# Two graph-attention layers on one core: the opening of the first group reordered, and three smaller edits

## The chip, the cores and the metric

The kernel runs on one core of one Trainium2 chip. The metric is the device time of one execution in microseconds. The profiler calls the engines PE (TensorE, matrix products), DVE (VectorE), ACT (ScalarE), POOL (GpSimd) and SP (SyncE, which here only issues DMAs). PEld is the loading of stationary weights into PE, which overlaps the products.

## The reference, cut to what matters

There are 64 graphs of 256 nodes with 512 features. Each of two layers normalizes, applies a relu, and adds what an attention over the same 256 x 256 adjacency returns.

```python
h = jnp.maximum(_layernorm(x), 0.0)
# layer 0: one head, 512 -> 256, output and h side by side
hw  = h @ W                                       # [64, 256, 256]
e   = leaky_relu(hw @ a[0] + swap(hw @ a[1]), 0.2)
e   = e + -1e9 * (1 - adj)
x   = x + concat([softmax(e) @ hw, hw], axis=-1)
h = jnp.maximum(_layernorm(x), 0.0)
# layer 1: eight heads of 64
q, k, v = h @ Wq.T + bq, h @ Wk.T + bk, h @ Wv.T + bv
s   = where(adj == 0, -inf, q @ k.T / 8)          # per head
x   = x + (softmax(s) @ v) @ Wo.T + bo
```

## The kernel before, in words

All data is float32. The 64 graphs are worked through in 32 groups of two graphs; a group is 512 rows, four strips of 128, two strips per graph. Python unrolls everything, so there are no loops on the chip.

A group passes four stages, each written as a generator whose `yield`s mark places where other work may be put in between.

- `first_norm(g)` takes the statistics of each strip (`st`, `mv`, on DVE), makes the factors `rstd` and `less` (a power and a product on POOL), writes the normalized strips `xn` (ACT, two buffers) and turns them. In the first group PE turns them (`pt`). In later groups DVE transposes 32 x 32 blocks into `xt`, of which there is one buffer, SP stores `xt` to DRAM as `passed`, and four fetches `moved` bring it back with the blocks rearranged. `put` copies the result into `hT0` on ACT.
- `first_layer(g)` multiplies by W with two extra columns for the attention scores (`ph`, copied to `H`), transposes one column of `H` (`pn`), builds the exponentials `e` and masks them with `maskT`, and multiplies by `H` (`po`, four strips). A last column of `H` that holds ones makes the row sums, so a reciprocal `ri` and one combine give the new half of x. Then it takes the statistics of the second normalization strip by strip and turns those strips in the same way, into `hT`; at its end POOL makes four `sums` of quarters of `hT`.
- `project(g)` makes q, k and v. Each is seven half-size products instead of eight (a Strassen-like scheme), so it needs `sums` and, once, sums of the weights (`weight_sums`, four DVE subtractions per matrix). It yields 21 times a group.
- `scores`, `weigh` and `outputs` do the eight-head attention and the last product.

Beside this, once, `judge()` bounds the scores from the inputs: it makes the gram matrices of Wq and Wk (`gram_q`, `gram_k`, 32 matmuls each), squares each three times, sums the squares of the other parameters on ACT, adds all up over the partitions (`total`), and writes one number, `wrong`; SP reads that number at the end of the program and would run a slower version for inputs that fail. `last_bias()` folds the bias of v through Wo into `b_out`, with a wide operand `bv_wide` made on POOL and eight matmuls `pb`; `residual(g)` adds `b_out` to x on POOL.

What sets the order: PE executes its instructions in the order of the program, since every product goes through `in_order` (L129 to L138). On the other engines a scheduler at compile time may move an instruction ahead of earlier ones, by its own model of when operands are ready; `not_sooner` (L121) forbids an instruction to stand ahead of the one written just before it on its engine, and does no more than that. Which piece of which stage is written next to which is fixed by hand: by the driver at L777 to L806 for the opening, where a string of letters says after each of the 21 products of the first group how many pieces of the second group's first layer (`s`) and of the following norms (`n`) come next, and by `steps` (L809) for all later groups. Nearly all instructions show line 35 (the helper that passes them on), 135 (products) or 138 (PE transposes) in the profile, so they are told apart by tile names. PSUM gives five rotating banks to `mm` and three held ones.

Loads of the first three groups' x and of all parameters are issued by SP in program order (L149 to L231). Eight buffers hold x.

Of the kernel before, what the change touches and what calls it, by code (L numbers as in the profile page):

```python
# [8 lines left out]
F32 = mybir.dt.float32  # L9
# [5 lines left out]
P = 128  # L15
# [42 lines left out]
def bounded(  # L58
# [48 lines left out]
    def mm(name):  # L107
        return psum.tile([P, 512], F32, tag="turn", name=name, bufs=5)
# [25 lines left out]
    def matmul(*args, **kwargs):  # L134
        in_order(nc.tensor.matmul(*args, **kwargs))  # L135
# [9 lines left out]
    def load(g, b):  # L145
        xs[g, b] = big.tile([P, NT, D], F32, tag="x", name=f"x{g}_{b}", bufs=8)
        nc.sync.dma_start(xs[g, b], xg[g, b])

    load(0, 0)  # L149
    load(0, 1)  # L150


    ident = const.tile([P, P], F32, name="ident")
    make_identity(nc, ident)

    w0_sb = const.tile([P, HP, F1 + 2], F32, name="w0_sb")
    nc.sync.dma_start(w0_sb[:, :, 2:], w0.rearrange("(c p) o -> p c o", p=P))
    maskT = const.tile([P, NT, N], F32, name="maskT")
    bad = const.tile([P, 2, NT], F32, name="bad")
    a_b = att.tile([P, 2, F1], F32, tag="ps", name="a_b", bufs=1)  # L160
    nc.sync.dma_start(
        a_b, bass.AP(tensor=a0.tensor, offset=a0.offset, ap=[[0, P], [F1, 2], [1, F1]])
    )
    adj_i = att.tile([P, NT, N], I32, tag="e", name="adj_i")
    nc.sync.dma_start(adj_i, adj.rearrange("(t p) k -> p t k", p=P))

    def score_columns():
# [6 lines left out]
                )  # L174

    def mask():
        edge = att.tile([P, NT, N], F32, tag="e", name="edge")
        vector.tensor_scalar(edge, adj_i, 0.0, None, op0=ALU.not_equal)
        pt = mm("pt_mask").rearrange("p (k q) -> p k q", k=NT)
        for kb in range(NT):  # L180
            for t in range(NT):
                transpose(
                    pt[:, kb, t * P : (t + 1) * P], edge[:, t, kb * P : (kb + 1) * P], ident
                )
        vector.tensor_copy(maskT, pt)

        vector.reduce_max(bad[:, 0, :], edge, axis=AX.X)
        vector.tensor_scalar(bad[:, 0, :], bad[:, 0, :], 0.0, None, op0=ALU.is_equal)
        vector.tensor_tensor(edge, edge, adj_i, op=ALU.not_equal)
        vector.reduce_max(bad[:, 1, :], edge, axis=AX.X)  # L190
# [53 lines left out]
    def last_bias():  # L244


        pb = mm("pb")
        b = att.tile([P, 2, 2, P], F32, tag="kept", name="bv_wide")
        for q in range(NQ):
            for half in range(2):  # L250
                gpsimd.tensor_scalar(
                    b[:, half, q, :], ones, bv_col[:, half, q : q + 1], None, op0=ALU.mult
                )
                matmul(
                    pb, b[:, half, q, :], w_sb["o"][:, half, 2 * q : 2 * q + 2, :],
                    start=(q == 0 and half == 0), stop=(q == NQ - 1 and half == 1),
                )
        vector.tensor_add(b_out, pb, b_out)


    def judge():
# [65 lines left out]
        yield  # L327
        yield from squares(2, *[w0_sb[:, c, 2:] for c in range(HP)])
        yield
        total = mm("total")[:, :10]  # L330
        matmul(total, ones, part, start=True, stop=True)
        norm = const.tile([P, 10], F32, name="norm")
# [140 lines left out]
    def first_norm(g):  # L473

        xt = {}
        mv = small.tile([P, GT, 2], F32, tag="mv", name=f"mv0_{g}")
        factors, norm, turn, fetch, put = norm_T(xt, mv, f"0_{g}", g == 0)
        for b in range(GB):
            for t in range(NT):
                xt[b * NT + t] = xs[g, b][:, t, :]  # L480
                stats(mv, xt, b * NT + t, f"0_{g}")
            factors(b)
            yield
            norm(b)
            yield
            turn(b)
            yield
            if g == 0:

                pool, tag, bufs = (big, "hT0", 1) if b == 0 else (att, "moved", 2)  # L490
                hT0[g, b] = pool.tile([P, HP, N], F32, tag=tag, name=f"hT0_{g}_{b}", bufs=bufs)
                put(b, hT0[g, b])
        if g == 0:
            return
        for b in range(GB):
            fetch(b)
        yield
        for b in range(GB):
            hT0[g, b] = big.tile([P, HP, N], F32, tag="hT0", name=f"hT0_{g}_{b}", bufs=1)
            put(b, hT0[g, b])  # L500
            yield

    def first_layer(g):

        xt = [xs[g, b][:, t, :] for b in range(GB) for t in range(NT)]

        H = big.tile([P, GT, F1 + 3], F32, tag="H", name=f"H_{g}", bufs=1)
        gpsimd.memset(H[:, :, F1 + 2 :], 1.0)
        for r in range(GT):
            b, t = divmod(r, NT)  # L510
            ph = mm(f"ph_{g}_{r}")[:, : F1 + 2]
# [28 lines left out]
        for r in range(GT):  # L540
            b, t = divmod(r, NT)
            po = mm(f"po_{g}_{r}")[:, : F1 + 1]
            for kb in range(NT):
                matmul(
                    po, pT[b][:, kb, t * P : (t + 1) * P], H[:, b * NT + kb, 2:],
                    start=(kb == 0), stop=(kb == NT - 1),
                )
            ri = small.tile([P, 1], F32, tag="ri", name=f"ri_{g}_{r}")
            vector.reciprocal(ri, po[:, F1:])
            vector.scalar_tensor_tensor(  # L550
                xt[r][:, :F1], po[:, :F1], ri, xt[r][:, :F1], op0=ALU.mult, op1=ALU.add
            )
            stats(mv, xt, r, f"1_{g}")
            if r == 1:
                factors(0)
            elif r == 2:
                norm(0)
            elif r == 3:
                factors(1)
                if g:  # L560
                    turn(0)
                    fetch(0)
            yield
# [19 lines left out]
    def residual(g):  # L583

        for b in range(GB):
            for t in range(NT):
                xt = xs[g, b][:, t, :]
                not_sooner(gpsimd, "tensor_add", xt, xt, b_out)
# [187 lines left out]

    verdict = judge()  # L777
    norms = (piece for g in range(NG) for piece in first_norm(g))
    for piece in range(5):
        next(norms)  # L780
        if piece == 2:
            score_columns()
    for piece, _ in enumerate(first_layer(0)):
        for _ in range((0, 2, 1, 2, 2, 1)[piece] if piece < 6 else 0):
            next(norms, None)
        if piece == 3:
            mask()
        elif piece == 4:
            next(verdict)
        elif piece == 9:  # L790
            last_bias()
        elif piece == 10:
            next(verdict)
        elif piece == 11:
            weight_sums("q")
    residual(0)
    products, pieces = project(0), first_layer(1) if NG > 1 else iter(())
    for i, parts in enumerate("n s s n s s s s s s s s s s nn nn nn s - - s".split()):
        next(products)
        if i in (1, 8, 15):  # L800
            weight_sums("kvo"[i // 7])
        for part in parts:
            if part != "-":
                next(norms if part == "n" else pieces, None)
        next(verdict, None)
    run(verdict)  # L806

# [402 lines left out]
```

## Time and profile before

| | us |
|---|---|
| median of 5 runs (2545.8 to 2549.89) | 2547.66 |
| the profiled execution, whole | 2549.75 |
| its span, first to last instruction | 2548.0 |
| PE busy in the span | 2511.2 |
| DVE / ACT / POOL busy | 1776.8 / 1006.5 / 956.4 |
| one group in the steady part (start of its first pq to that of the next, 192.10 to 269.39) | 77.3 |

The span is what the profile covers; the whole execution has 1.75 us around it. Busy times are sums over instructions. The opening, up to about 130 us, is where the groups fill the pipeline; after it each group repeats the same order every 77.3 us. Times in the text are microseconds from the span's start. In the prediction a row "A <- B" of a waits view says that A's engine stood idle until B, with the total, the number of times and the longest; in a view by time a row begins with its start and duration, and brackets at its end give the idle time before it and what ended that.

### The profile page before, as it was taken

How to read it: one execution, taken by the hardware profiler on the slowest of the kernel's cores; microseconds unless marked ns; L12 is line 12 of the kernel's file. 1: busy time of each engine (PE TensorE's matmuls, PEld its weight loads, DVE VectorE, ACT ScalarE, POOL GpSimd, SP SyncE). 2: the span in 40 equal slices, each digit the busy share in tenths (PEclk: the TensorE clock that was granted, in tenths of full speed). 3: DMA queues.
4: the chain of work that ended last, by engine and by line, in shares of the span. 5: the costliest groups of instructions: out<-in, count | busy, mean ns of one | idle time of the engine just before them, and what ended most of it. 6: DMA issues, size and time to landing. Idle time of an engine off the chain costs nothing.

```text
span 2548.0 us, 41575 instructions
## 1 busy us (share of the span) xinstructions
PE 2511.2 (99%) x16158; PEld 2029.5 (80%) x16158; DVE 1776.8 (70%) x2975; ACT 1006.5 (40%) x2015; POOL 956.4 (38%) x944
## 2 busy tenths in 40 slices
PE   7899999999999999999999999999999999999998
PEld 5788888887888888888788888878888888887875
DVE  5667667767677776677776677776677676777655
ACT  3444343433433433434433434344334434334321
POOL 2334343333443333443243433334433334432332
PEclk8999999999999999999999999999999999999999
DMA  6111222312323212223212233123233123232110
GB/s 186 61 65 60 90 83 92 100 59 67 100 75 100 91 59 75 92 83 100 78 60 87 83 92 100 59 67 100 75 100 97 56 73 98 77 100 81 37 34 34
DMA packets 129353, 205.40 MB, mean 81 GB/s; under 512 B 13952, under 2 KB 78208, under 8 KB 129152
## 3 DMA queue, kind: packets, MB, share of 16 engines
q1 hardware_dynamic: 129152, 202.69, 25.4%
q8 instruction: 129, 2.11, 0.4%
q14 instruction: 72, 0.59, 0.1%
HBM read 104.08 MB, written 98.57 MB: 80 GB/s over the span
## 4 chain that ended last, share of the span: by engine, by line
PE 96%; DVE 2%; ACT 1%; POOL 1%; DMA 1%; issue 0%; SPq 0%; ACTq 0%; DVEq 0%; POOLq 0%
PE pq L135 15%; PE pv L135 15%; PE pk L135 15%; PE py L135 15%; PE sc L135 10%; PE ph L135 9%; PE pr L135 9%; PE po L135 4%; PE total L135 3%; PE pn L138 1%; DMA x<-in_x_dram 0%; DMA a_b<-in_L_gnn_a_dram 0%; DVE p L35 0%; POOL ps L35 0%; DVE st L35 0%
## 5 line engine op out<-in xcount | busy, mean ns | idle before, releaser
L35 POOL TENSOR_TENSOR ps<-p 128x512 f32<-128x512 f32 x256 | 416.4, 1641 | 697.0 <-DVE p L35 697.0
L35 DVE TENSOR_TENSOR x<-py,x 128x256 f32<-128x256 f32 x448 | 186.5, 416 | 314.1 <-PE py L135 307.4
L35 ACT ACTIVATE p<-sc 128x512 f32<-128x512 f32 x512 | 264.3, 603 | 272.5 <-PE sc L135 272.5
L35 DVE TENSOR_TENSOR p<-p,maskT 128x1024 f32<-128x1024 f32 x256 | 335.7, 1341 | 48.8 <-ACT p L35 48.8
L35 ACT ACTIVATE xn<-x,less,rstd 128x512 f32<-128x512 f32 x256 | 194.9, 812 | 323.0 <-POOL less L35 307.1
L135 PE MATMUL sc<-q,k 64*128 64x256 f32 x2048 | 266.9, 390 | 0.0
L135 PE MATMUL py<-wo_sb,o_sums 128*128 128x256 f32 x1024 | 262.7, 380 | 2.6 <-DVE x L35 2.6
L35 DVE RECIPROCAL r<-total 128x256 f32<-128x256 f32 x128 | 224.7, 1755 | 44.6 <-PE total L135 44.6
L135 PEld LDWEIGHTS sc<-q,k 64*128 64x128 f32 x2048 | 195.9, 186 | 72.2 <-issue 52.6
L135 PE MATMUL ph<-w_sb,hT 128*128 128x258 f32 x1024 | 245.6, 387 | 1.7 <-ACT hT L35 1.3
L135 PE MATMUL pr<-p,v 128*32 128x256 f32 x4096 | 245.5, 379 | 0.0
L135 PE MATMUL pv<-wv_sb,sums 128*128 128x256 f32 x1024 | 241.8, 379 | 1.2 <-ACT kept_v L35 1.2
L135 PE MATMUL pq<-sums,wq_sb 128*128 128x256 f32 x1024 | 238.5, 381 | 3.0 <-POOL sums L35 3.0
L35 POOL TENSOR_TENSOR rstd<-ve,rexp 128x2 f32<-128x2 f32 x128 | 90.1, 704 | 401.7 <-DVE less L35 401.7
L135 PE MATMUL pk<-sums,wk_sb 128*128 128x256 f32 x1024 | 240.2, 382 | 0.0
L135 PEld LDWEIGHTS ph<-w_sb,hT 128*128 128x128 f32 x1024 | 193.3, 192 | 41.1 <-ACT p L35 9.9
L135 PEld LDWEIGHTS pk<-sums,wk_sb 128*128 128x128 f32 x1024 | 191.7, 190 | 35.6 <-issue 10.3
L135 PEld LDWEIGHTS pq<-sums,wq_sb 128*128 128x128 f32 x1024 | 195.2, 191 | 30.3 <-POOL sums L35 3.8
L135 PEld LDWEIGHTS pv<-wv_sb,sums 128*128 128x128 f32 x1024 | 194.5, 190 | 28.0 <-ACT kept_v L35 1.6
L135 PEld LDWEIGHTS py<-wo_sb,o_sums 128*128 128x128 f32 x1024 | 191.9, 190 | 29.1 <-DVE x L35 3.4
L135 PEld LDWEIGHTS pr<-p,v 128*32 128x32 f32 x4096 | 134.6, 110 | 86.7
L135 PE MATMUL py<-wo_sb,oT 128*128 128x256 f32 x768 | 197.0, 380 | 2.5 <-DVE x L35 2.5
(120 smaller groups left out, 3729.1 us busy)
## 6 DMA issues: line engine op xcount, KB each, us to landing
passed<-xt SPq DMA_DIRECT2D x124, 512.0 KB, 2.7
moved<-passed SPq DMA_DIRECT2D x496, 128.0 KB, 3.5
x<-in_x_dram SPq DMA_DIRECT2D x64, 512.0 KB, 4.8
out_dram<-x SPq DMA_DIRECT2D x64, 512.0 KB, 3.8
wq_sb<-in_L_gnn_Wq_dram SPq DMA_DIRECT2D x2, 512.0 KB, 9.7
wk_sb<-in_L_gnn_Wk_dram SPq DMA_DIRECT2D x2, 512.0 KB, 12.5
wo_sb<-in_L_gnn_Wo_dram SPq DMA_DIRECT2D x8, 128.0 KB, 8.6
wv_sb<-in_L_gnn_Wv_dram SPq DMA_DIRECT2D x2, 512.0 KB, 6.3
```

What stands on the lines that cost most here:

```text
L35: instruction = getattr(self.engine, operation)(*args, **kwargs)
L135: in_order(nc.tensor.matmul(*args, **kwargs))
L138: in_order(nc.tensor.transpose(*args))
```

## The change

There are six edits.

1. The load of the second half of the first group's x goes behind those of the score vectors (`a_b`) and of W (`w0_sb`). The adjacency tiles `adj_i` and `edge` use the buffers with the tag "kept" instead of "e".
2. Both grams of `judge()` are written behind the exponentials of the first group, so both are ahead of `po` on PE; before, the second stood after `pb` and the first transposes. `total` comes three steps later.
3. `last_bias()` becomes a generator in three pieces: the wide operand on POOL is written with the grams, `pb` stays behind `po`, and the add to `b_out` comes two pieces later, bound to the order written.
4. The reciprocal of each `po` strip, in all groups, is bound behind the DVE instruction written before it. In the first group that one is a transpose of the second group, or the reciprocal's own predecessor strip.
5. The first `residual` goes from ahead of the first product to behind product 15, and the string that mixes the second and third group's pieces with the products is another one: several first-layer pieces come in pairs, and the third group's norm starts two steps sooner.
6. `H` is one tile for the whole program, and its column of ones is written once instead of once per group.

```diff
     load(0, 0)
-    load(0, 1)
...
-    w0_sb = const.tile([P, HP, F1 + 2], F32, name="w0_sb")
-    nc.sync.dma_start(w0_sb[:, :, 2:], w0.rearrange("(c p) o -> p c o", p=P))
     maskT = const.tile([P, NT, N], F32, name="maskT")
...
-    adj_i = att.tile([P, NT, N], I32, tag="e", name="adj_i")
+
+    w0_sb = const.tile([P, HP, F1 + 2], F32, name="w0_sb")
+    nc.sync.dma_start(w0_sb[:, :, 2:], w0.rearrange("(c p) o -> p c o", p=P))
+    load(0, 1)
+    adj_i = att.tile([P, NT, N], I32, tag="kept", name="adj_i")
...
-        edge = att.tile([P, NT, N], F32, tag="e", name="edge")
+        edge = att.tile([P, NT, N], F32, tag="kept", name="edge")
...
     def last_bias():
-        pb = mm("pb")
-        b = att.tile([P, 2, 2, P], F32, tag="kept", name="bv_wide")
+        wide = att.tile([P, 2, 2, P], F32, tag="kept", name="bv_wide")
         for q in range(NQ):
             for half in range(2):
                 gpsimd.tensor_scalar(
-                    b[:, half, q, :], ones, bv_col[:, half, q : q + 1], None, op0=ALU.mult
-                )
+                    wide[:, half, q, :], ones, bv_col[:, half, q : q + 1], None, op0=ALU.mult
+                )
+        yield
+        pb = mm("pb")
+        for q in range(NQ):
+            for half in range(2):
                 matmul(
-                    pb, b[:, half, q, :], w_sb["o"][:, half, 2 * q : 2 * q + 2, :],
+                    pb, wide[:, half, q, :], w_sb["o"][:, half, 2 * q : 2 * q + 2, :],
                     start=(q == 0 and half == 0), stop=(q == NQ - 1 and half == 1),
                 )
-        vector.tensor_add(b_out, pb, b_out)
+        yield
+        not_sooner(vector, "tensor_add", b_out, pb, b_out)
+        yield
...
         yield from squares(2, *[w0_sb[:, c, 2:] for c in range(HP)])
         yield
+        for _ in range(3):
+            yield
         total = mm("total")[:, :10]
...
+    H = const.tile([P, GT, F1 + 3], F32, name="H")
+    gpsimd.memset(H[:, :, F1 + 2 :], 1.0)
+
     def first_layer(g):
...
-        H = big.tile([P, GT, F1 + 3], F32, tag="H", name=f"H_{g}", bufs=1)
-        gpsimd.memset(H[:, :, F1 + 2 :], 1.0)
...
-            vector.reciprocal(ri, po[:, F1:])
+            not_sooner(vector, "reciprocal", ri, po[:, F1:])
...
+    bias = last_bias()
...
     for piece, _ in enumerate(first_layer(0)):
+        if piece == 4:
+            next(verdict)
+            next(verdict)
+            next(bias)
         for _ in range((0, 2, 1, 2, 2, 1)[piece] if piece < 6 else 0):
             next(norms, None)
         if piece == 3:
             mask()
-        elif piece == 4:
-            next(verdict)
         elif piece == 9:
-            last_bias()
-        elif piece == 10:
-            next(verdict)
+            next(bias)
         elif piece == 11:
+            next(bias)
             weight_sums("q")
-    residual(0)
     products, pieces = project(0), first_layer(1) if NG > 1 else iter(())
-    for i, parts in enumerate("n s s n s s s s s s s s s s nn nn nn s - - s".split()):
+    order = "n s s n ss s s - ss ss s s n n n s n n n - s"
+    for i, parts in enumerate(order.split()):
         next(products)
         if i in (1, 8, 15):
             weight_sums("kvo"[i // 7])
         for part in parts:
             if part != "-":
                 next(norms if part == "n" else pieces, None)
+        if i == 15:
+            residual(0)
         next(verdict, None)
     run(verdict)
```

## The prediction

> **What bounds the kernel now.** I read the engine shares first, then busy time by stretch, then TensorE's waits in the opening, then that stretch in order of time.
>
> The page, engine shares:
>
> ```profile
> PE 2511.2 (99%) x16158; PEld 2029.5 (80%) x16158; DVE 1776.8 (70%) x2975; ACT 1006.5 (40%) x2015; POOL 956.4 (38%) x944
> ```
>
> PE idles 2548.0 - 2511.2 = 36.8 us in all. Busy time by stretch (stretch, its length, then busy us of PE, PEld, DVE, ACT, POOL, granted clock, DMA share, GB/s):
>
> ```profile
> 0.00:8.57 8.57, 0.00 (x0) 0.00 (x0) 2.32 (x10) 2.15 (x3) 1.93 (x14) 1.00 0.69 216
> 8.57:24.00 15.43, 13.70 (x48) 10.13 (x49) 8.30 (x32) 6.38 (x12) 3.84 (x7) 1.00 0.94 288
> 24.00:31.00 7.00, 4.62 (x41) 4.43 (x40) 6.88 (x17) 3.48 (x9) 1.54 (x3) 1.00 0.52 77
> 31.00:39.26 8.26, 5.40 (x17) 4.12 (x17) 6.27 (x21) 1.34 (x2) 1.66 (x5) 0.77 1.03 385
> 39.26:46.00 6.74, 6.67 (x8) 2.34 (x8) 0.12 (x2) 0.00 (x0) 2.59 (x5) 0.52 0.10 38
> 46.00:56.00 10.00, 7.69 (x50) 7.03 (x50) 2.75 (x5) 4.51 (x7) 0.00 (x0) 0.83 0.62 157
> 90.00:130.00 40.00, 32.33 (x147) 26.53 (x146) 24.96 (x67) 19.65 (x48) 15.62 (x17) 0.96 0.34 106
> 130.00:2433.80 2303.80, 2303.80 (x14934) 1866.35 (x14932) 1634.71 (x2701) 928.52 (x1848) 878.71 (x861) 1.00 0.26 81
> ```
>
> From 130 to 2433.8 us PE never idles, and its last 114 us hold the same work either way. So the change can win or lose only in the first 130 us, or by breaking that unbroken stretch. What idles there (PE's waits, 80 to 140 us):
>
> ```profile
> PE total L135 <- DVE part L35: 3.5, 1, 3.5
> PE pq L135 <- POOL sums L35: 3.0, 1, 3.0
> PE pv L135 <- ACT kept_v L35: 1.2, 1, 1.2
> ```
>
> The opening in order of time (start, duration), which shows what blocks the first projection, pq:
>
> ```profile
> 24.88 3.74 PE L135 MATMUL gram_q<-wq_sb 128*128 128x128 f32 x32
> 31.02 5.39 PE L135 MATMUL po<-H,e 128*128 128x257 f32 x16 [2.40 <-DVE e L35]
> 39.26 7.12 PE L135 MATMUL pb<-wo_sb,bv_wide 128*128 128x512 f32 x8 [2.84 <-POOL bv_wide L35]
> 48.69 1.82 PE L138 MATMUL pt<-ident,xn 128*128 128x128 f32 x8 [2.31 <-ACT xn L35]
> 50.30 4.81 PE L135 MATMUL gram_k<-wk_sb 128*128 128x128 f32 x32
> 55.83 1.89 PE L135 MATMUL pq<-hT,wq_sb 128*128 128x256 f32 x8
> ```
>
> And the DMA view of the one `passed` store issued at 29.62 (last number: us from issue to landing):
>
> ```profile
> passed<-xt SPq DMA_DIRECT2D x1, 512.0 KB, 10.0
> ```
>
> pq starts at 55.83, behind the wide product pb, the b_out add (46.41), the second group's transposes (47.02 to 48.31), xn (47.82), pt and gram_k. The store lands 10.0 us after its issue, at 39.6; that row decides the new opening.
>
> **The change part by part.**
>
> *Load order.* Ahead of a_b stand x(0,0) and x(0,1) and w0; afterwards only x(0,0). x(0,0) lands at 4.6, x(0,1) at 5.8, so a_b (10.34 now) and the score columns behind it come about 1.3 us earlier; SP's later loads keep their place and the DMA engines are full anyway (0.94). adj and edge on "kept" free the first e from waiting 2.9 us for the adjacency check. Both speed up only what ends in another wait (next item), so I count zero; bounds -1.3 and +1 (x(0,1) now lands later, and its statistics with it).
>
> *Both grams ahead of po.* gram_k (32 matmuls, 3.74 at full clock by gram_q's row) fills the 2.40 idle; po then starts near 31 as now, but with PE busy before it, at full clock: 16 x 0.26 (1.03 for 4) = 4.1 instead of 5.39. wk landed at 21.6, so nothing is waited for. *bv_wide* (4 x 0.606 on POOL, inputs landed by 27.5) runs before po ends, delaying only POOL's norm factors, which have slack; pb then ends near 39. The b_out add (0.69) moves behind the last factors, where no one waits for it. No gain by itself: the end of this stage is set by DVE.
>
> *Transposes pinned ahead of the reciprocals.* The xt buffer is single: transposes of the second group's second half wait until the store of the first half has landed, 39.6. Now the four reciprocals, ready to run from 32, stand behind that on DVE, and the statistics, factors and xn behind them. From there: transposes 1.29, to 40.9; four strips of reciprocal, combine, statistics and aggregate at 0.21 + 0.59 + 0.73 + 0.09 = 1.62 (starts at 32.16, 32.37, 32.96; statistics to aggregate 4.63 to 5.36, aggregate to reciprocal 36.59 to 36.68), to 47.4; ve and less 0.35; POOL's power and product 1.15 (37.44 to 38.59); xn 1.52; put 1.05; 0.2 of starts: pq at 51.7. Against 55.83: **-4.1**. Bounds by rows: if the store lands in 3.0 us, like the second one, -11; if only with the last x load at 41.9, -1.8.
>
> *Clock.* PE is now idle from about 39 to 46.5. After the idle of 2.31 at 46.38 the clock was 0.50 until about 52.5; each low spell here lasted about 3.4 or 6.9 us. pq therefore starts cold: half of up to 5 us: **+1.5** (0 to +2.5).
>
> *weight sums, residual.* Sums of wq took 4 in 4.77 us beside POOL adds, those of wo 4 in 2.86 alone. The residual (4 adds, 6.76 beside DVE, 4.96 mostly alone) leaves the first place and lands on the second, after product 15. Then DVE pays up to 1.9 more and the third group's rstd waits behind POOL; PE waits for neither directly. Zero; bounds 0 and +1.9. SBUF — State Buffer (section "SBUF: two separate sides") of the Trainium skill says that of a DVE operation with two SBUF inputs and a GpSimd one, the later to start is blocked for the whole instruction. The sums' 1.19 against 0.72 us agree in sign; full blocking would put rstd behind the whole overlap, 6.8 + 4.8 us by these rows, and cost +2 rather than zero.
>
> *Verdict three steps later, pieces in pairs.* `total` waits 3.5 us for ACT's squares (94.22 to 98.3). The squares now follow the xn of the second group's second half, because that piece moved from step 12 to 10. Carrying PE's own durations (1.73 a product, 0.89 a square, 1.74 a ph strip, 0.87 a po strip) from a warm start at 53.2, `total` comes up near 97.1; the reciprocals, behind the wv sums (2.8 us), end near 91.4, xn near 94.3, the squares near 98.3. So 1.4 to 1.9 us of wait remain: **-1.8** (-3.5 to 0).
>
> *Sums of the second group.* put(1) and the sums sat behind the third group's xn on ACT (116.22 to 119). That norm comes two to three steps earlier; by the same carrying, s2 ends at 110.5 to 111.4 and its product comes up at 112 to 113. The 2.98 wait goes, and with it the clock drop behind it: 24 pq matmuls took 7.17 from 122.88, against 24 x 0.2165 = 5.2 at full clock: **-4.7** (-4.7 to 0; the latter if SP's read of the verdict, which held SP 4.6 us from 98.03 with the fetches behind it, keeps its place while the verdict comes later). TensorE: Matmul & The Clock Gate (Part 1) of the Trainium skill puts the drop after an idle window of about 3.4 us. Here 2.40 and 2.98 us of idle were followed by 0.50, while 3.50 us at 95.09 were not, so the rows go against a fixed length; by the rule that item would be -2.98.
>
> *kept_v.* The third group's xn now stands at step 13, ahead of the copy of the first pv. If ACT takes them in that order, the copy waits: today such an order costs 1.19. Zero change; bounds -1.2 and +5.7 (xn ready near 100.7, done 102.2, copy 102.8, against 97.1).
>
> *H set once.* 31 memsets of 0.10 us and their waits (7.3 us in the first group, 0.7 in each other) leave POOL, which nothing on PE awaits: zero. *Pinned reciprocals later:* in the steady period they already follow their predecessors (316.19 behind the k add, 318.69 and 322.55 behind x adds): zero; bounds 0 and +0.68 a group, one such add.
>
> Sum: -4.1 + 1.5 - 1.8 - 4.7 = **-9.1**. The profiled execution took 2549.75 (span 2548.0 and 1.75 around it), 2.1 above the median of 2547.66; it becomes 2540.7, and the median 2538.6, given as 2538.5.
>
> **The rivals.**
> 1. *Everything clears.* total, kept_v and sums wait nowhere and pq is warm: -4.1 - 3.5 - 1.2 - 4.7 = -13.5: 2534.2. For it: the waits are single events with slack of a few us. Against: the squares' order.
> 2. *A new wait for an old one.* ACT blocks kept_v behind xn: -9.1 + 5.7 = -3.4: 2544.3. For it: xn waited for POOL 3.71 at 106.84 with kept_v behind it. Against: kept_v is not pinned and may be placed ahead.
> 3. *Slower: the pin breaks the steady stretch.* If a pinned reciprocal holds a PSUM bank for one more add, 0.68 x 31 = 21.1 - 9.1 = +12: 2559.7. It turns the sign from 0.29 us a group on. Against: the order just read, and DVE at 70%.
> 4. *Nothing happens, near 2546:* the store lands after 43.7 and the waits merely move. Against: all loads are down by 41.9.
>
> **How the numbers follow.** A measurement of this kernel can tell about 0.2%, 5.1 us, from no change. Forecast 0.45, rival 1 0.20, rival 2 0.15, rival 3 0.12, rival 4 0.08. Faster: 0.45 + 0.20 and a little of rival 2, 0.67; same: the rest of rival 2 and rival 4, 0.20; slower 0.13. Range 2533 to 2548: it takes in rival 1, 2 and 4 and leaves out rival 3 and the far low end.
>
> **What the next profile would show.** Right: gram_k directly after gram_q, po without a wait of 2.4; xt transposes near 39.6 with DVE idle before them, released by `passed`; the first reciprocal after 40.9; pq near 51.7 and cold; `total` waiting under 2 us; no wait of pq for sums; a period of still 77.3. Wrong: transposes well before or after 39.6, a wait at pv above 2 us, any PE wait after 130 us.

## The result and the profile after

The changed kernel takes 2542.85 us (median of 21 runs, 2540.44 to 2544.50); the kernel before took 2548.36 beside it (41 runs). The ratio is 0.9977, 95% interval 0.9971 to 0.9983, so 5.9 us less, between 4.3 and 7.4. The forecast was 9.1 less. The profiled execution has a span of 2542.9 against 2548.0; both profiled executions are slower than their medians (2544.78 and 2549.75).

The page of the changed kernel, engine shares:

```profile
PE 2506.2 (99%) x16158; PEld 2027.6 (80%) x16158; DVE 1771.2 (70%) x2975; ACT 1006.5 (40%) x2015; POOL 954.3 (38%) x913
```

PE now idles 2542.9 - 2506.2 = 36.7 us, as much as before (36.8). The products are the same, so PE is busy 5.0 us less because, on balance, less of them runs at half clock. Busy time by stretch (stretch, its length, then busy us of PE, PEld, DVE, ACT, POOL, granted clock, DMA share, GB/s):

```profile
38.00:46.90 8.90, 0.00 (x0) 0.00 (x1) 6.07 (x18) 0.87 (x2) 0.92 (x2) 0.77 0.83 273
46.90:52.00 5.10, 3.37 (x15) 2.97 (x16) 4.64 (x10) 2.93 (x5) 1.16 (x2) 0.50 0.33 66
52.00:57.00 5.00, 5.00 (x19) 4.16 (x18) 0.00 (x0) 2.12 (x6) 3.66 (x3) 0.55 0.00 0
90.00:100.00 10.00, 7.61 (x28) 6.05 (x27) 7.28 (x25) 5.97 (x19) 1.80 (x4) 0.83 0.23 82
130.00:2433.80 2303.80, 2303.80 (x14919) 1866.92 (x14912) 1637.28 (x2704) 929.50 (x1848) 875.22 (x832) 1.00 0.26 81
```

The last row is the unbroken stretch: 2303.80 of 2303.80 us, and a group still takes 77.3 us (187.22 to 264.52). From about 130 us on the two executions differ by 0.3 us; all else lies ahead of that. There PE does nothing at all for 8.9 us ahead of 46.90, then works at 0.50 and 0.55 of the clock, and drops again between 90 and 100. What it waits for up to 140 us:

```profile
PE pt L138 <- ACT xn L35: 20.4, 4, 9.1
PE pk L135 <- ACT kept_k L35: 2.4, 1, 2.4
PE total L135 <- DVE part L35: 1.1, 1, 1.1
PE pv L135 <- DVE v L35: 0.4, 1, 0.4
PE pq L135 <- POOL sums L35: 0.2, 1, 0.2
```

And the row of the kernel before that the forecast does not show:

```profile
PE pt L138 <- ACT xn L35: 10.9, 2, 8.6
```

`total` fell from 3.5 to 1.1, `sums` from 3.0 to 0.2, kept_v is gone (1.2); a wait of 2.4 for kept_k is new, and PE's wait for xn grew from 10.9 to 20.4 (8.6 and 8.2 of it stand at the very start of the span, for the first load of x). The same in order of time:

```profile
23.56 3.74 PE L135 MATMUL gram_q<-wq_sb 128*128 128x128 f32 x32
27.13 3.74 PE L135 MATMUL gram_k<-wk_sb 128*128 128x128 f32 x32
30.70 3.64 PE L135 MATMUL po<-H,e 128*128 128x257 f32 x16
34.18 3.60 PE L135 MATMUL pb<-wo_sb,bv_wide 128*128 128x512 f32 x8
46.90 1.97 PE L138 MATMUL pt<-ident,xn 128*128 128x128 f32 x8 [9.13 <-ACT xn L35]
50.59 1.97 PE L138 MATMUL pt<-ident,xn 128*128 128x128 f32 x8 [1.73 <-ACT xn L35]
52.35 3.67 PE L135 MATMUL pq<-hT,wq_sb 128*128 128x256 f32 x8
...
57.04 1.89 PE L135 MATMUL pq<-hT,wq_sb 128*128 128x256 f32 x8
...
93.94 3.68 PE L135 MATMUL pk<-hT,wk_sb 128*128 128x256 f32 x8 [2.39 <-ACT kept_k L35]
...
128.64 0.64 PE L135 MATMUL total<-ps,ones 128*32 128x256 f32 x8
```

The first pq starts 3.48 us earlier than before (55.83) but takes 3.67 in place of 1.89, and the second pq is only 1.41 ahead (58.45 before). The last row is the first group's softmax sums, which share the name `total`: 133.44 before, so 4.80 is gained by then, and the spans differ by 5.1. The ledger of these two executions: up to the second pq -1.41, of which 1.32 is there already when gram_q starts (24.88 before, 23.56 now); `total` -2.39; kept_v to v -0.84; sums -2.76 and the clock drop behind them -1.8; kept_k +2.39 and the half clock behind it +1.79. That is -5.02.

### The profile page after: what moved, and what is told of

Same layout as the page of the kernel before. It is cut to its first block, busy times and chain, and to the rows that moved or that the text cites. A ratio compares the mean times of both kernels' runs of the same rounds, so it can differ in the third digit from the quotient of the medians.

```text
span 2542.9 us, 41535 instructions
## 1 busy us (share of the span) xinstructions
PE 2506.2 (99%) x16158; PEld 2027.6 (80%) x16158; DVE 1771.2 (70%) x2975; ACT 1006.5 (40%) x2015; POOL 954.3 (38%) x913
## 4 chain that ended last, share of the span: by engine, by line
PE 95%; DVE 1%; DMA 1%; POOL 1%; SPq 0%; ACT 0%; issue 0%; DVEq 0%; ACTq 0%
PE pq L135 15%; PE pk L135 15%; PE pv L135 15%; PE py L135 15%; PE sc L135 10%; PE ph L135 9%; PE pr L135 9%; PE po L135 4%; PE total L135 3%; PE pn L138 1%; DMA x<-in_x_dram 0%; DMA passed<-xt 0%; DMA wo_sb<-in_L_gnn_Wo_dram 0%; DVE p L35 0%; POOL ps L35 0%; POOL sums L35 0%
```

## The experiments

All times are medians, the ratio is to the kernel before on the same chip, with its 95% interval. Runs on different chips are compared by these ratios. "Forecast" is the prediction above. The last two columns come from the one profiled execution of each kernel: "opening" runs from the start of gram_q to that of the second pq, "middle" from there to the first group's softmax sums. What follows the middle takes 2414.1 to 2414.6 us in all fourteen, and what stands ahead of gram_q 22.51 to 25.22.

| kernel | us | ratio | opening | middle |
|---|---|---|---|---|
| before | 2548.36 | 1 | 33.57 | 74.99 |
| changed | 2542.85 | 0.9977 (0.9971 to 0.9983) | 33.48 | 71.60 |
| before + H set once | 2548.03 | 0.9998 (0.9989 to 1.0007) | 32.06 | 74.96 |
| before + pinned reciprocals | 2545.28 | 0.9991 (0.9982 to 1.0000) | 29.56 | 76.51 |
| before + new string, residual, later `total` | 2545.34 | 0.9989 (0.9980 to 0.9998) | 33.31 | 71.84 |
| changed, opening in its old places | 2536.99 | 0.9957 (0.9943 to 0.9970) | 28.96 | 70.67 |
| changed, old string | 2549.02 | 1.0002 (0.9993 to 1.0011) | 33.30 | 78.18 |
| changed, old string and residual in front | 2548.65 | 1.0004 (0.9995 to 1.0013) | 32.63 | 76.67 |
| changed, `total` three steps sooner | 2548.46 | 1.0000 (0.9991 to 1.0009) | 32.33 | 77.54 |
| changed, reciprocals free | 2541.52 | 0.9969 (0.9958 to 0.9979) | 29.15 | 70.86 |
| changed, second buffer for xt | 2535.30 | 0.9945 (0.9932 to 0.9959) | 24.43 | 70.94 |
| changed, wv sums at product 11 | 2544.42 | 0.9986 (0.9977 to 0.9995) | 32.11 | 72.19 |
| second buffer and wv sums at 11 | 2536.59 | 0.9959 (0.9945 to 0.9973) | 24.41 | 72.18 |
| second buffer and wv sums at 5 | 2534.49 | 0.9941 (0.9927 to 0.9954) | 24.43 | 72.01 |

### H set once, alone

```diff
+    H = const.tile([P, GT, F1 + 3], F32, name="H")
+    gpsimd.memset(H[:, :, F1 + 2 :], 1.0)
     def first_layer(g):
...
-        H = big.tile([P, GT, F1 + 3], F32, tag="H", name=f"H_{g}", bufs=1)
-        gpsimd.memset(H[:, :, F1 + 2 :], 1.0)
```

> The kernel before with one edit alone: H one tile, its ones written once. Theory A: nothing on PE waits for it, time as before within 1 us. Rival (POOL, freed of the memset's 7.3 us wait in the first group, moves the opening): 2 us or more faster.

2548.03, ratio 0.9998: no change, as the forecast's zero. This run has a second use. But for the memset of H on POOL its opening is that of before, and its profiled execution reads differently from that of before. Its grams and products around po:

```profile
23.47 3.74 PE L135 MATMUL gram_q<-wq_sb 128*128 128x128 f32 x32
29.60 3.71 PE L135 MATMUL po<-H,e 128*128 128x257 f32 x16 [2.40 <-DVE e L35]
36.59 6.96 PE L135 MATMUL pb<-wo_sb,bv_wide 128*128 128x512 f32 x8 [3.28 <-POOL bv_wide L35]
...
52.91 1.89 PE L135 MATMUL pq<-hT,wq_sb 128*128 128x256 f32 x8
```

The first gram starts at 23.47 in place of 24.88, po takes 3.71 in place of 5.39 after the very same wait of 2.40, and pq stands at 52.91, not 55.83. The memset is not there, and no run tells its part in this. But the ten kernels that share the changed kernel's code ahead of gram_q start it anywhere between 22.51 and 25.22, and the four with the old loads between 23.47 and 24.88. So the start of gram_q in one execution tells little about an edit, the order of the loads included, and I measure the opening from gram_q on.

Five kernels have the changed opening up to the second pq (the changed one, both with the old string, `total` sooner, wv sums at 11): 32.11 to 33.48. Three have the old one without the pin: 32.06 to 33.57. By these rows no gain of the new opening can be told. Of the 5.9 us the middle accounts for 3.4; whether any of the rest comes from the opening stays open.

### The old places of the opening

```diff
-        if piece == 4:
-            next(verdict)
-            next(verdict)
-            next(bias)
         for _ in range((0, 2, 1, 2, 2, 1)[piece] if piece < 6 else 0):
             next(norms, None)
         if piece == 3:
             mask()
+        elif piece == 4:
+            next(verdict)
         elif piece == 9:
-            next(bias)
+            for _ in bias:
+                pass
+        elif piece == 10:
+            next(verdict)
         elif piece == 11:
-            next(bias)
             weight_sums("q")
```

> Changed kernel with the second gram, the wide operand, pb and the b_out add back in their old places of the opening; the string, the pinned reciprocals, the loads and H as changed. Theory A (the early grams lose the cover that the second gram gave to the wait for xn, so TensorE idles 9 us and starts cold; with the old places, as in the kernel before with the pin alone, pq starts 26.9 us after the first gram, warm, against 28.8 and half clock): the second pq comes 3.5 to 4 us earlier against the first gram, and the time is 2538.5 to 2541. Rival B (the early grams gain what was forecast, 2.6 us net): 2544.5 to 2547. Rival C (the gain in the opening is taken back by a longer wait at kept_k or total): 2542 to 2544.

2536.99, ratio 0.9957: theory A, and more than it asked. By the ratios this is 0.0020 of the time, 5.1 us, under the changed kernel. PE in order of time:

```profile
28.82 3.71 PE L135 MATMUL po<-H,e 128*128 128x257 f32 x16 [1.55 <-POOL less L35]
35.20 5.47 PE L135 MATMUL pb<-wo_sb,bv_wide 128*128 128x512 f32 x8 [2.68 <-POOL bv_wide L35]
42.98 1.97 PE L138 MATMUL pt<-ident,xn 128*128 128x128 f32 x8 [2.31 <-ACT xn L35]
44.74 4.42 PE L135 MATMUL gram_k<-wk_sb 128*128 128x128 f32 x32
...
49.87 1.89 PE L135 MATMUL pq<-hT,wq_sb 128*128 128x256 f32 x8
```

gram_q started at 23.53. PE waits three times for 1.55 to 2.68 us here and not once for 9, and gram_k spends the low clock that pq pays in the changed kernel. The second pq comes at 52.49, 28.96 after gram_q against 33.48: 4.5 us by these two traces, and 3.1 against the shortest of the five changed openings. What makes the difference on DVE is the place of the reciprocals. In this kernel, DVE:

```profile
29.96 0.17 DVE L35 RECIPROCAL ri<-po 128x1 f32<-128x1 f32 x1
...
40.71 0.69 DVE L35 TENSOR_TENSOR b_out<-pb,b_out 128x512 f32<-128x512 f32 x1 [3.72 <-PE pb L135]
41.31 1.29 DVE L35 STREAM_TRANSPOSE xt<-xn 128x512 f32<-128x512 f32 x2
```

and in the changed kernel:

```profile
30.91 0.69 DVE L35 TENSOR_TENSOR room<-gram_k,room 128x512 f32<-128x512 f32 x1 [0.94 <-PE gram_k L135]
40.24 1.31 DVE L35 STREAM_TRANSPOSE xt<-xn 128x512 f32<-128x512 f32 x2 [8.64 <-DMA passed<-xt]
41.47 0.13 DVE L35 RECIPROCAL ri<-po 128x1 f32<-128x1 f32 x1
```

A pinned reciprocal stands behind the DVE instruction written just before it. With the grams in their old place that is the product `room<-gram_q` on DVE, which is soon done, and the statistics of all four strips run from 30 to 37 while the store is under way. With the grams written first, it is the second group's transposes, and the statistics run after the store. The transposes stand near 41 in both; what costs is the work that is tied behind them. In the old opening the pin holds nothing up; in the new one it does.

### Reciprocals free

```diff
-            not_sooner(vector, "reciprocal", ri, po[:, F1:])
+            vector.reciprocal(ri, po[:, F1:])
```

> The changed kernel with the reciprocals free again, all else kept. Theory A (the pin makes the ready reciprocals stand behind the store of the first transposed half, which lands near 40): without it the four reciprocals run between 31.5 and 39, the transposes follow behind them, and pq starts near 47 instead of 52.35; the whole execution is 4 to 6 us below the changed kernel, near 2538. Theory B (the pin is what brought the gain, since transposes that stand behind the reciprocals hold the two xn buffers and so the first group's own normalization): pq starts later than 52.35 and the time goes back up, to 2546 or more.

2541.52, ratio 0.9969; the span is 2537.3. The reciprocals go at 30.92 and pq starts at 48.60 (2.52 for 8), and the second pq comes 29.15 us after gram_q (51.85 - 22.70) against 33.48. So the tie to the transposes costs the opening 4.3 us (3.0 against the shortest of the five). With the grams early and the tie undone the opening is as short as with the grams in their old places (28.96): of the two causes that the forecast of that run names, it is the tie that costs, not the lost cover. In the middle a wait of pv for `v` of 3.33 appears at 105.89, which the changed kernel has at 0.35; there `total` no longer waits and kept_k waits 1.90 without a clock drop, and in sum the middle is 0.7 us shorter. Yet by the ratios the whole time is only 2.0 us shorter, and the intervals overlap. Against the kernel before, opening and middle of this run add up to -8.5 and the ratio says -7.9; for the changed kernel they add up to -3.5 and the ratio says -5.9. It is the profiled execution of the changed kernel that does not fit, slower than all of its 21 runs. So the pin, booked at zero, costs the opening 3 to 4 us; how much of that the whole time shows is not settled.

### A second buffer for xt

```diff
-            xt = att.tile([P, J, HP, NT, S], F32, tag="xt", name=f"xt{name}_{b}", bufs=1)
+            tag, bufs = ("moved", 2) if (name, b) == ("0_1", 1) else ("xt", 1)
+            xt = att.tile([P, J, HP, NT, S], F32, tag=tag, name=f"xt{name}_{b}", bufs=bufs)
```

> The changed kernel; only the second group's second transposed half gets another buffer (one of the two of 'moved', idle then), so nothing waits for the store's landing and the pinned order is kept. Theory A: the 8.6 us idle of DVE before the transposes goes, transposes near 30.5, reciprocals from 32, pq near 43.5, 8 to 9 us earlier; some of it is lost to a colder clock or to later waits, so 6 to 9 us below the changed kernel, near 2535. Rival: the transposes wait for xn or for DMA traffic anyway, pq moves by less than 2 us, time within 2 us of the changed kernel's.

2535.30, ratio 0.9945: faster than both kernels, 8.2 us under the changed one by the ratios. The transposes start at 30.47 and wait for no store, the reciprocals follow at 31.69, and PE runs:

```profile
40.97 1.04 PE L138 MATMUL pt<-ident,xn 128*128 128x128 f32 x8
42.56 1.36 PE L138 MATMUL pt<-ident,xn 128*128 128x128 f32 x8 [0.55 <-ACT xn L35]
44.22 1.99 PE L135 MATMUL pq<-hT,wq_sb 128*128 128x256 f32 x8 [0.29 <-ACT hT L35]
```

The long wait for xn is gone, pq starts warm, and the second pq comes 24.43 us after gram_q (46.94 - 22.51) against 33.48. That shows the store of the one xt buffer as the limit of the changed opening, as the forecast's item on the transposes reads it.

### The pin alone, and the string alone

In before, the pin alone:

```diff
-            vector.reciprocal(ri, po[:, F1:])
+            not_sooner(vector, "reciprocal", ri, po[:, F1:])
```

> Kernel before with the reciprocals pinned, nothing else. Theory A (the pin alone puts the first group's reciprocals behind the second group's transposes, which wait for the store to land near 39.6; with the old place of gram_k and pb in front, PE then has work to 46 and pq moves little): pq between 50 and 54, time 2544 to 2549. Rival B (the pin is what gains the opening, by putting transposes, reciprocals and xn in the order pq needs): pq near 51.7, time 2543 to 2545. Rival C (pin loses: the bv_wide and gram_k pieces come behind the late statistics): above 2550. In the steady stretch no wait of PE in any of them.

2545.28, ratio 0.9991: 2.3 us, at the edge of what can be told. pq starts at 50.47, warm, 26.94 after gram_q, and the opening is 29.56 long in place of 33.57. Here the strips' statistics follow one another on DVE, bv_wide is made in one piece, and pb starts 13.36 after gram_q in place of 14.38 and at full clock (4.00 for 7.12). `total` waits 4.97 in place of 3.50, with half clock behind it (pk 3.76 for 8), and takes a part back.

Set side by side, four openings say what the change did. Old places and free reciprocals take 32.06 to 33.57 us, old places with the pin 28.96 and 29.56, early grams with free reciprocals 29.15, and early grams with the pin 32.11 to 33.48. Either edit alone goes with an opening that is 2.5 to 4.6 us shorter; together they give nothing, because the early grams change what the pin ties to. (One or two executions stand behind each but the first and the last, and the runs cut down from the changed kernel have its loads and its H too.)

In before, the new string with the residual behind product 15 and the three extra steps before `total`, and no other edit:

```diff
+        for _ in range(3):
+            yield
         total = mm("total")[:, :10]
...
-    residual(0)
-    for i, parts in enumerate("n s s n s s s s s s s s s s nn nn nn s - - s".split()):
+    order = "n s s n ss s s - ss ss s s n n n s n n n - s"
+    for i, parts in enumerate(order.split()):
...
+        if i == 15:
+            residual(0)
```

> Kernel before with the new string of pieces, the residual behind product 15 and the three extra steps ahead of total; the opening, the loads, H and the reciprocals as before. Theory A (the whole measured gain comes from the middle; the opening's earlier pq is spent on the cold clock, and the changed opening with the old string measured no gain): 2541.5 to 2544, with the wait for sums below 0.5. Rival B (the string gains only with the new opening or the pinned reciprocals in front): 2545.5 to 2549.

2545.34, ratio 0.9989, 2.8 us: between the two expectations. `total` and `sums` wait nowhere, so the string does clear the two waits that the forecast gave it, alone. But kept_k waits 1.92 and `v` 3.34. The middle is 71.84 long, as in the changed kernel (71.60), with the opening of before. The two single edits give 5.1 us in sum; together with the load order and H, in the old opening, they give 11 (0.9957). Neither edit's worth can be read from the other's absence.

### The old string in the changed kernel

```diff
-    order = "n s s n ss s s - ss ss s s n n n s n n n - s"
+    order = "n s s n s s s s s s s s s s nn nn nn s - - s"
```

> The changed kernel with the old string of pieces (residual still behind product 15, verdict still three steps later). Theory A (the pairs bring ACT's xn ahead of the kept_k copy, 2.39 us of wait and 1.8 us of half clock; the earlier third-group norm removed the wait for the second group's sums, 3.0 us and 1.8 us of half clock): the kept_k wait goes and the sums wait comes back in part; time within 3 us of the changed kernel, the two waits trading places. Rival (the string as a whole costs): 4 us or more faster. Rival (the string as a whole is what gains): 4 us or more slower.

2549.02, ratio 1.0002: the whole gain is gone, 6.4 us. The waits for kept_k and `total` vanish with it, but pq waits 6.85 for `sums` (3.0 before the change) and 24 pq matmuls behind it take 7.19; pv also waits 1.72 for the k add and 2.26 for kept_v (1.19 before). To see whether the residual's new place makes this, it went back to the front:

```diff
-    order = "n s s n ss s s - ss ss s s n n n s n n n - s"
+    order = "n s s n s s s s s s s s s s nn nn nn s - - s"
+    residual(0)
...
-        if i == 15:
-            residual(0)
```

> Changed kernel with the old string of pieces and with the residual back ahead of the first product: the order of the middle as before, the opening as changed. Theory A (with the old string alone the sums of the second group waited 6.85 us because the residual, after product 15, stood ahead of them on GpSimd): with the residual in front the wait of pq for sums is back at about 3.0 us with a cold stretch of 1.8 behind it, and the time lies between the changed kernel and the one with the old string alone, near 2545 (2543 to 2547). Rival B (SyncE's read of the verdict holds the fetches of the third group, and the place of the residual does not matter): the wait stays above 5 us and the time is 2548 to 2550.

2548.65, ratio 1.0004: rival B's time, and theory A falls. The wait for sums is 4.38, not the 3.0 of theory A and not above 5 as rival B had it; between these two profiled executions the residual made 2.5 us of it, between the medians nothing that can be told. The trace puts what is left of the wait on SP's queue (the last row is SP's own wait, at the read of the verdict):

```profile
99.99 0.38 SPq L434 DMA_DIRECT2D passed<-xt  x1
109.54 1.73 SPq L441 DMA_DIRECT2D moved<-passed  x4
...
SPq L51 <- DVE wrong L35: 8.2, 1, 8.2
```

The fetches `moved` are issued 9.6 us after the store. Between them SP reads `wrong`, which DVE writes at 108.4 (the read starts at 108.6). In the changed kernel the store is at 101.57 and the fetches at 104.28. So with the later `total` the old string puts the read in front of the third group's fetches; the new string takes the fetches ahead of it. This is the case that the forecast named under the bound of zero for the sums. No run moved the read alone.

### `total` three steps sooner

```diff
-        for _ in range(3):
-            yield
         total = mm("total")[:, :10]
```

> Changed kernel without the three extra steps ahead of total, nothing else. In the changed kernel total starts at 103.91 after a wait of 1.11. Theory A (the squares on ScalarE that total needs stay where they are, near 103.5, so each step that total stands earlier is waited for): total waits 4 to 7 us with a half-clock stretch behind it perhaps, later waits shrink by a part of it, and the time is 2546 to 2549. Rival B (ScalarE has room and takes the squares earlier as well, or the later waits for kept_v, v and sums take back the whole wait): within 1.5 us of the changed kernel, 2541.5 to 2544.

2548.46, ratio 1.0000. The wait of `total` is 4.80 in place of 1.11, with a clock drop behind it:

```profile
102.92 0.57 PE L135 MATMUL total<-part,ones 128*128 128x10 f32 x2 [4.80 <-DVE part L35]
103.34 3.76 PE L135 MATMUL pk<-sums,wk_sb 128*128 128x256 f32 x8
106.90 4.23 PE L135 MATMUL pv<-wv_sb,hT 128*128 128x256 f32 x16
```

Wait +3.7, pk at 3.76 for 1.89 and pv at 4.23 for 3.62, together +2.5; by the ratios the times differ by 5.9. `total` comes up at 98.1 in place of 102.8, and the last square ends at 102.6 in place of 103.7: the squares come only a microsecond sooner. The three steps are worth all of the gain: without them the change would have measured nothing.

### The new wait for kept_k

ACT in the changed kernel, around the copy that frees PE's bank:

```profile
91.04 1.52 ACT L35 ACTIVATE xn<-x,less,rstd 128x512 f32<-128x512 f32 x2 [3.80 <-POOL less L35]
92.46 0.61 ACT L35 ACTIVATE squares<-wv_sb 128x512 f32<-128x512 f32 x1
...
93.07 0.81 ACT L35 ACTIVATE kept_k<-pk,bk_sb 128x256 f32<-128x256 f32 x2
```

xn waits 3.80 for its factors, and kept_k, whose product PE finished at 91.5, stands behind it and a square. The factors are late because DVE takes the four wv sums (83.61, 2.93 us) ahead of the first reciprocal (86.46). So the wv sums were moved from product 8 to product 11:

```diff
-        if i in (1, 8, 15):
-            weight_sums("kvo"[i // 7])
+        if i in (1, 11, 15):
+            weight_sums({1: "k", 11: "v", 15: "o"}[i])
```

> Changed kernel with the weight sums of wv called at product 11 instead of product 8, nothing else. Theory A (the new wait of pk for kept_k, 2.39 us, with 1.8 us of half clock behind it, comes from the pinned reciprocals that stand behind the 2.9 us of wv sums on VectorE, which make xn late on ScalarE, which stands ahead of the kept_k copy): the wait is gone or below 0.5, no cold stretch after it, and the time is 2538.5 to 2540 against 2542.9. Rival B (ScalarE's order alone makes the wait, xn is as late without the sums, or the sums at 11 delay the next copy): the wait stays at 2 or moves to pv or total, and the time is within 1.5 us of the changed kernel.

2544.42, ratio 0.9986: not faster. The wait for kept_k is gone, and pv waits for the k add instead, which now stands behind the sums on DVE:

```profile
PE pv L135 <- DVE k L35: 3.1, 1, 3.1
PE pv L135 <- DVE v L35: 1.4, 1, 1.4
```

The wv sums were a cause of the wait, and the gain was not there. The pin, which theory A names with them, is not needed: with free reciprocals the sums and the strips' work take turns on DVE, and kept_k still waits 1.90, and 1.92 with the string alone. The same edit on top of the second xt buffer:

> Changed kernel with the second half of the second group's xt in a buffer of its own (tag moved) and the weight sums of wv at product 11. If the two causes are separate, their gains add: 2535.3 less about 4, so 2531 to 2532, with pq near 44 and no wait of pk for kept_k. Rival: with the opening earlier, PE reaches the same copies sooner and the gain of the second edit is lost in a wait at total or at pv: 2534 to 2536.

2536.59, ratio 0.9959: no better than the buffer alone (0.9945). pv waits 3.10 for the k add and 1.37 for `v` again. Product 5 instead, where DVE idles:

```diff
-        if i in (1, 8, 15):
-            weight_sums("kvo"[i // 7])
+        if i in (1, 5, 15):
+            weight_sums({1: "k", 5: "v", 15: "o"}[i])
```

> Changed kernel with the second half of the second group's xt in a buffer of its own, and the weight sums of wv at product 5, where VectorE idles, instead of product 8. Theory A (the wait for kept_k, 2.39 us with 1.8 of half clock, comes from the wv sums that hold up the pinned reciprocals; at product 11 they held up the k add instead; at product 5 they hold up nothing): no wait at kept_k and none at pv above 0.5, 2531 to 2533 against 2535.3 with the buffer alone. Rival B (the gain is lost in the wait for total or for sums, whose sources do not come sooner): 2534.5 to 2536.5.

2534.49, ratio 0.9941: the lowest time of all, but not to be told from the buffer alone (0.9945). kept_k waits nowhere, and theory A falls on its second half: pv waits 3.36 for `v` at 100.80. POOL in this run:

```profile
90.52 6.31 POOL L35 TENSOR_TENSOR x<-x,b_out 128x512 f32<-128x512 f32 x4
96.80 2.41 POOL L35 TENSOR_TENSOR norm<-norm,power 128x10 f32<-128x10 f32 x1
```

and DVE beside it and behind it:

```profile
91.02 1.32 DVE L35 TENSOR_TENSOR wo_sb<-wo_sb 128x512 f32<-128x512 f32 x1
...
92.38 1.64 DVE L35 TENSOR_TENSOR wo_sb<-wo_sb 128x512 f32<-128x512 f32 x1
...
94.55 1.16 DVE L35 TENSOR_TENSOR wo_sb<-wo_sb 128x512 f32<-128x512 f32 x1
...
96.30 1.08 DVE L35 TENSOR_TENSOR wo_sb<-wo_sb 128x512 f32<-128x512 f32 x1
...
99.24 0.16 DVE L35 TENSOR_TENSOR test<-norm 128x1 f32<-128x1 f32 x1 [1.76 <-POOL norm L35]
...
100.05 0.69 DVE L35 TENSOR_TENSOR v<-pv,kept_v 128x512 f32<-128x512 f32 x1
```

The v add stands behind the verdict's tests, those wait for POOL's norm, and that stands behind the residual. What differs from the changed kernel is when the residual runs, seen from `total`. There it starts 2.6 us ahead of `total` (101.27 and 103.91) and takes 4.96; here it starts 0.4 behind it (90.52 and 90.14) and takes 6.31, because all four sums of wo run beside it (1.32, 1.64, 1.16 and 1.08 us in place of 1.17, 0.67, 0.68 and 0.68). So 3.0 us of the delay are its place and 1.35 the overlap. In the run with free reciprocals and in the one with the string alone the residual starts with `total` and takes 6.32, and the wait is 3.3 as here; with the wv sums at product 11 alone it starts 2.5 ahead and takes 5.41, and the wait is 1.37. So one wait covers the next one; what a place for the residual ahead of product 15's sums would bring was not tried.

## Why the prediction was right, and where not

The forecast was 2538.5 with 2533 to 2548 around it; 2542.85 lies in that range, on its upper half, and the sign is right. The time lies between the forecast and rival 2 (2544.3), and the largest of what parts it from the forecast is rival 2's mechanism, at another copy. That the number fell so near rival 2's is luck: its price was 5.7 for kept_v, and kept_k cost 4.2. By the ledger the other parts are an opening that gave 1.2 us less than forecast, and `total` and kept_v, which gave 0.6 and 0.8 more.

- *Both grams ahead of po.* As described: gram_k at 27.13, po at 30.70 without a wait in 3.64 (4.1 forecast), pb done at 37.8 (39). "No gain by itself" was wrong both ways: with free reciprocals the early grams go with an opening of 29.15 in place of 32.06 to 33.57, and with the pin the old places measure 5.1 us better, since the early grams change what the pinned reciprocals are tied to.
- *Transposes pinned ahead of the reciprocals, -4.1.* Every step of the working is in the trace: the store is issued at 30.66, DVE idles 8.64 until it has landed, transposes at 40.24 (39.6 forecast), the first reciprocal at 41.47, pq at 52.35 (51.7). As a place of pq it was off by 0.65, and the four other executions of that opening have pq at 51.21 to 52.94. As a gain it failed: it was taken against 55.83, a place that one execution gave, while the string alone has 54.66 and H alone 52.91 with the old order. 1.3 us of it lay in a later start of gram_q.
- *Clock, +1.5.* Right: pq takes 3.67 for 1.89 and the square behind it 1.38 for 1.05. By the starts, +2.07.
- Together the opening was to bring -2.6; the two profiles show -1.41, of which -0.1 lies behind the start of gram_q. Against H set once alone it is +1.4 there.
- *Load order, H, residual.* H measured 0. The load order was not run alone. In the old places with the pin po starts 5.29 after gram_q with the new loads and tags and 6.14 with the old ones, and the second pq 0.6 us sooner, one execution each. The residual cost nothing in the changed kernel itself, but the upper bound of that item (+1.9) was passed, with 3.3 us, in the three runs just named, mostly because it starts later against `total`, and for 1.35 us because the sums of wo fall beside it. SBUF — State Buffer (section "SBUF: two separate sides") of the Trainium skill says that of a DVE operation with two SBUF inputs and a GpSimd one that reads SBUF, whichever starts first holds the shared ports for its whole instruction, and the other is blocked. The trace agrees, instruction by instruction: with the wv sums at product 5 the residual's four adds end at 91.80, 93.47, 95.15 and 96.83, and each of the four sums starts during one of them and ends 0.54 to 0.56 us after it. The forecast took the block for a whole series (6.8 + 4.8); the two series take turns, and take 6.3 in place of 4.96 and 5.2 in place of 3.2.
- *Verdict three steps later, -1.8.* It measured -2.39 in the wait, and 1.11 of waiting is left where 1.4 to 1.9 was forecast. Its worth against leaving it out is 5.9, since the squares are late in the new string too.
- *Sums of the second group, -4.7.* Right: the wait is 0.22, the clock drop is gone, -4.56 together. The reason given for the bound of zero, SP's read of the verdict ahead of the fetches, is what happens with the old string.
- *kept_v, zero, bounds -1.2 and +5.7; rival 2.* The step that failed. The mechanism, an xn on ACT ahead of the copy that frees PE's bank, was priced at the third group's xn and kept_v, and there the wait shrank by 0.84. It struck earlier, at the second group's xn and kept_k, with 2.39 of wait and 1.79 of half clock, +4.18. The forecast had carried the reciprocals "behind the wv sums" and the xn behind them to 94.3, and did not ask which copy stood behind that xn on ACT. With this term the middle's -6.5 becomes -3.2, kept_v included (measured -3.4, from -1.41 at the second pq to -4.80).
- *Pinned reciprocals, zero; rival 3.* In the steady stretch right: no wait of PE after 130 us, period 77.3. In the opening the pin is the tie described above: some 4 us gained in the old order, 3 to 4 lost in the new one.
- *Rival 1* had the waits of the middle cleared at once, and the runs show why that does not come easily: each wait removed exposed the next (kept_k, the k add, `v`). *Rival 4* fell, the store landed in time.

## What to carry to other kernels

Before an instruction is bound to "the one written before it", look up which one that is after every other edit has moved: here one and the same pin tied four short reciprocals to a DVE product that was soon done, or to a transpose that waited 8.6 us for a store, and two edits that each went with an opening some 3 to 4 us shorter gave nothing together. Measure a place in an opening from an event ahead of the change and in more than one execution, since the start and the clock shift it by as much as the edit may bring. And for every step that is moved earlier, list what stands behind it on each engine it uses, copies that free PSUM first; then ask of each removed wait which other delay it was hiding.

## What the hardware showed beyond expectation

The clock does not drop after a fixed idle time. 2.39 us at kept_k were followed by half clock in the changed kernel (3.68 for 8 matmuls), 1.92 in the run with the string alone were not (1.99), and 3.50 at `total` were not in two executions of the old middle (1.97). The wait for `v` of 3.3 was followed by half clock in the string alone (2.48 for 8, then 3.15 for 16) and with the wv sums at product 5 (3.78 and 3.19), and not with free reciprocals (1.99 and 2.00). In the clock records of the fourteen traces every change inside the span lies a whole number of steps of 3.41 us from the others, and every low spell but the last of a span, which its end cuts, lasts 3.41, 6.83 or 13.65 us; the long one is the one behind PE's 9.1 us of idle. TensorE: Matmul & The Clock Gate (Part 1) of the Trainium skill describes a free-running window of about 3.4 us and a count of slow matmuls that varies from run to run; the step of 3.41 us and the readings on both sides agree with that. By the table there in the Trainium skill the clock falls after at least one idle window of that length. As a threshold for a single wait that does not hold here: 2.39 us were enough.
